# A graph network on one core: where the deferred rows of the second stage are kept, and the order in which its queues load and store at the start

## The chip, the core and the metric

The kernel runs on one of the eight cores of a Trainium2 chip. The metric is the device time of one execution in microseconds; a version is judged by the median of several executions. The core has five engines with an instruction queue each: TensorE (matmuls; PE in the profile), VectorE (DVE), ScalarE (ACT), GpSimd (POOL) and SyncE (SP), which here only issues transfers. SP, ACT and POOL can all issue transfers.

## What is computed

There are 10,000 nodes with 512 features and 160,000 edges, sorted by target, of four types. Two graph layers are computed, each with a normalised input and a residual:

```python
h = relu(layernorm(x))
# layer 0
msg = (einsum('nd,rdf->nrf', h, rel_W) + rel_b)[src, edge_type]
agg = segment_sum(msg, dst) / max(deg, 1)
x1  = layer_norm(h + h @ self_W + self_b + agg) * ln1_w + ln1_b
f   = gelu(x1 @ W1 + b1) @ W2 + b2
x   = x + layer_norm(x1 + f) * ln2_w + ln2_b
# layer 1: two SAGE layers on h = relu(layernorm(x))
h = relu(h @ W_self1 + mean_of_neighbours(h) @ W_neigh1 + b1)
h = relu(h @ W_self2 + mean_of_neighbours(h) @ W_neigh2 + b2)
x = x + h
```

W1 is 512 x 1024 and W2 is 1024 x 512. The call to `setup_inputs()` gives random features, edges and weights.

## The kernel before

Nodes are worked on in 79 blocks of 128 rows (`P`); the last block, 78, has 16 rows. There are four stages, each of them one loop over the blocks.

The **message stage** (lines 585 to 820) computes for each pair of blocks the four messages of every node and stores them in `hall_d`. It also computes the self term `h @ self_W + self_b` (with the identity added to the weights, so that it holds the residual too) and stores it in `xs_d`. For 24 blocks, 52 to 75, listed in `late`, the self term is not computed there: `residual` (line 698) stores the transposed block to `hT_d` instead (line 705), and the next stage makes up for it. Lists of edges are made beside this stage, on all engines, in pools of their own.

The **feed-forward stage** (from line 912, in `aligned`) is the middle one and the subject of this document. For each block it gathers rows of messages by indirect transfers from GpSimd (line 844, 256 KB each): up to 5 "others" tiles which TensorE adds up through 0/1 matrices (`hots`, `sums`, line 897), and 11 "mine" tiles, which VectorE adds one after the other (line 908). Blocks that begin a span of 4 or 16 blocks gather another tile, a tail; it is split into an upper and a lower half by VectorE and ScalarE (`halves_of`, lines 834 to 837). Every gathered tile comes from one ring of 28 tiles, `row_tile()`. A tile of the ring can be written again when its last use in program order is done.

After the sums of a block come its scale and residual (line 1181), its statistics, the first normalisation (lines 1081 to 1088), and the transposition for the feed-forward product (line 1016). The feed-forward products run one group of blocks behind: block 78 is a group, then groups of four. A group's 8 "up" slices (line 1028, then a Gelu on ScalarE into `hid`, line 1030) and its "down" products (line 1039) are put into `queue`, and one part of it is worked off in each round of the block loop, between the sums of two blocks. So the first two rounds have no feed-forward products to do.

The **deferred rows** are put into this gap. `fetch(n)` loads the next n blocks of `hT_d` (line 968), each into one tile of the ring. `residuals(n)` multiplies the oldest n of those loaded by `wself` (line 977, 4 matmuls of 512 columns each, which appear as 8 instructions in the trace), adds the bias on VectorE in place (line 979) and stores the row to `xs_d` (line 980). `LATE` says how many are fetched at each of its calls: the first two before the loop, the others in rounds 0 to 4. `ready` holds the ones that were fetched in the current round, which are left for the next one; `products` (line 1142) begins with two deferred rows, then does the part of the queue with the transposition in its middle, and ends with the rest of the rows.

The order of the work is the program's order on every engine: `aligned` runs under a manual schedule, each engine's queue is worked off in order, and waits are put in where tiles are written, read and used again. The transfers of SyncE are one such queue: a store that waits for its result holds back every load behind it. Before the loop, SyncE's order is: four deferred rows, the first two blocks of `xs_d`, the four stores of deferred rows, constants (`ln1w`, `lnb2`, `b2s` and two columns), four more deferred rows, `w1s`, `b1s`, `ln2w`. `w2s` is loaded in round 1.

Memory: the pools of a stage are laid out one after the other above the constants, on the place of the pools of the stage before: the ring `gat`, the weights `wp2`, the stage's tiles `gp` (with `hid`, 16 KB a partition, among them), and small ones, `sp`.

The **last two stages** (from line 1212) are the two SAGE layers, with the same gathers from `h1_d` and `h2_d`. The first of their gathers needs every row of `h1_d`, so it begins when the feed-forward stage has stored its last block.

Of the kernel before, what the change touches and what calls it, by code (L numbers as in the profile page):

```python
# [16 lines left out]
P = 128  # L17
# [4 lines left out]
def kernel(  # L22
# [789 lines left out]
    def aligned(ctxa):  # L812
# [98 lines left out]
        with ExitStack() as s:  # L911
            ring.append((s.enter_context(tc.tile_pool(name="gat", bufs=1)), RINGS[0]))
            wp = s.enter_context(tc.tile_pool(name="wp2", bufs=1))
            gp = s.enter_context(tc.tile_pool(name="gp", bufs=1))
            sp = s.enter_context(tc.tile_pool(name="sp", bufs=3))
            psT = s.enter_context(tc.tile_pool(name="psT2", bufs=1, space=PSUM))
            psC = s.enter_context(tc.tile_pool(name="psC", bufs=1, space=PSUM))
            psH = s.enter_context(tc.tile_pool(name="psH", bufs=2, space=PSUM))
# [36 lines left out]
                                  allow_slow_non_contiguous=True)  # L955
                return t

            LATE = (4, 4, 4, 3, 3, 3, 3)
            assert sum(LATE) == len(late)
            halves = [wself[:, :2], wself[:, 2:]]  # L960
            waiting, arrived = list(late), []

            def fetch(n):

                for b in waiting[:n]:
                    i = late.index(b)
                    t = row_tile()
                    nc.sync.dma_start(t, hT_d[i * P:(i + 1) * P, :])
                    arrived.append((b, t))
                del waiting[:n]  # L970

# [8 lines left out]
                    nc.sync.dma_start(xs_d[b * P:(b + 1) * P, :], t)  # L980
                del arrived[:n]

            fetch(LATE[0])
            for b in blocks[:2]:
                load(b)
            lanes = psC.tile([P, D], F32, name="lanes")[:, :P]
            nc.scalar.copy(lanes, lane)
            first_hot = hots(blocks[0], gp, lanes)
            residuals(LATE[0])
            ln1w = wide(wp, ln1_w, D, "ln1w")  # L990
            lnb2 = wide(wp, ln1_b, D, "lnb2")
            b2s = gp.tile([P, 2, D], F32, name="h1", bufs=2)[:, 0, :]
            nc.sync.dma_start(b2s, bass.AP(tensor=b2.tensor, offset=b2.offset,
                                           ap=[[0, P], [1, D]]))
            ln1wc, ln1bc = column(ln1_w, "ln1wc"), column(ln1_b, "ln1bc")
            fetch(LATE[1])
            nc.sync.dma_start(w1s, w1.rearrange("(k p) n -> p k n", p=P))
            nc.sync.dma_start(b1s, b1.rearrange("(f p) -> p f", p=P),
                              allow_slow_non_contiguous=True)
            ln2w = wide(wp, ln2_w, D, "ln2w")  # L1000
            taken = []

            class Group:
# [18 lines left out]
                def up(self, f):  # L1022
                    n = len(self.bs) * self.r
                    if self.hid is None:
                        self.hid = gp.tile([P, FC, 4 * P], F32, name="hid")
                    ph = psH.tile([P, 4 * P], F32, name="ph")
                    for k in range(KC):
                        nc.tensor.matmul(ph[:, :n], w1s[:, k, f * P:(f + 1) * P],  # L1028
                                         self.xT[:, k, :n], start=(k == 0), stop=(k == KC - 1))
                    nc.scalar.activation(self.hid[:, f, :n], ph[:, :n], AF.Gelu,  # L1030
                                         bias=b1s[:, f:f + 1], scale=1.0)
# [109 lines left out]
            def products(work, turned):  # L1141


                nonlocal fed
                got = []
                residuals(2)
                for i, call in enumerate(work):
                    if i == len(work) - 1:
                        yield
                    if i == len(work) // 2 and turned:  # L1150
                        turned()
                    got.append(call())
                if not work:
                    yield
                    if turned:
                        turned()
                residuals(len(arrived) - len(ready))
                fed = [g for g in got if g]
# [3 lines left out]
            for bs in plan:  # L1162
                for b in bs:
# [6 lines left out]
                        hot = hots(blocks[i + 1], gp, lanes)  # L1170
                    ready = []
                    if i + 2 < len(LATE):
                        fetch(LATE[i + 2])
                        ready = arrived[-LATE[i + 2]:]
                    if i == 1:
                        nc.sync.dma_start(w2s, w2.rearrange("(k p) n -> p k n", p=P))
                    got = second()
# [424 lines left out]
```

## Time and profile before

| | us |
|---|---|
| median of the runs | 7042.43 (7034.37, 7042.43, 7061.51) |
| the profiled execution | 6174.73 |
| its span, first to last instruction | 6172.9 |
| TensorE busy in it | 5643.4 |
| GpSimd busy (gathers) | 3722.7 |
| VectorE busy | 3671.8 |
| ScalarE busy | 1799.6 |
| last matmul of the message stage begins | 1206.43 |
| first gather of the feed-forward stage begins | 1206.87 |
| its last gather begins | 2853.8 |
| first gather of the next stage begins | 2949.35 |

The profiled execution is 868 us shorter than the median of the runs; nothing in the page says where the others spend that time. Durations below are those of the profiled execution.

The page gives for each engine the time it is busy, and for each group of instructions a mean duration and the idle time before it with the one who ended it. A matmul instruction that is busy may still be slow: the rate that the clock's throttle granted stands in a row of its own. Time of GpSimd is the time in which it makes the list for one gather; the data land later (3.8 us at the median). "Idle before" of an engine costs only where the engine, or one that waits for it, sets the end.

### The profile page before, as it was taken

The page shows a single profiled execution, that of the slowest core. Times are in us where ns is not written, and L with a number is a line of the kernel's source. Part 1 is how long each engine was busy: PE and PEld are TensorE (multiplying, and loading weights), DVE is VectorE, ACT ScalarE, POOL GpSimd, SP SyncE. Part 2 cuts the span into 40 slices and gives each one's busy share as a digit, 9 for nine tenths or more (in the row PEclk, how much of TensorE's full clock was granted, in tenths as well). Part 3 has the DMA queues.
Part 4 walks back from the last instruction along what each step waited for, and adds up shares of the span by engine and source line. Part 5 has one row for each costly group of instructions (what it writes and reads, how often), then busy time and mean ns, then how long its engine had stood idle before and what let it go on. Part 6 is the DMA issues. An engine that isn't in the chain of part 4 may idle for free.

```text
span 6172.9 us, 55148 instructions
## 1 busy us (share of the span) xinstructions
PE 5643.4 (91%) x15103; PEld 2563.5 (42%) x15103; DVE 3671.8 (59%) x7447; ACT 1799.6 (29%) x3594; POOL 3722.7 (60%) x3927
## 2 busy tenths in 40 slices
PE   9999999989999999999788888888878888888888
PEld 4555554444444444444333333333333333333333
DVE  8889999467877777775343434434334444444444
ACT  1026665013333333333222222222222222222222
POOL 0001110167777777773677777777767777777776
PEclk9999999999999999999999999999999999999999
DMA  4333344388888888885777777777778787888887
GB/s 161 116 124 128 122 145 150 139 282 253 263 259 262 262 253 258 253 260 164 232 235 238 234 238 234 237 237 235 238 235 251 246 251 247 250 251 246 251 246 218
DMA packets 503502, 1373.79 MB, mean 223 GB/s; under 512 B 82206, under 2 KB 82206, under 8 KB 503054
## 3 DMA queue, kind: packets, MB, share of 16 engines
q0 software_dynamic: 308768, 1008.91, 54.7%
q1 hardware_dynamic: 193886, 360.20, 16.0%
q8 instruction: 122, 2.00, 0.1%
q14 instruction: 198, 1.62, 0.1%
q10 hardware_dynamic: 528, 1.05, 0.0%
HBM read 1156.54 MB, written 213.30 MB: 222 GB/s over the span
## 4 chain that ended last, share of the span: by engine, by line
PE 40%; DMA 39%; DVE 8%; issue 6%; POOL 5%; ACT 1%; SPq 0%; POOLq 0%; DVEq 0%; ACTq 0%
DMA rows<-h_d,row 21%; PE pm L774 15%; DMA rows<-h_d,orow 13%; PE pa L897 6%; PE ph L1028 6%; POOL rows L844 5%; PE po L1039 5%; DMA rows<-hall_d,row 3%; DVE pa L908 3%; PE pm L678 2%; PE po L1273 1%; PE po L977 1%; PE pT L172 1%; DVE st L1066 1%; PE po L1244 1%
## 5 line engine op out<-in xcount | busy, mean ns | idle before, releaser
L908 DVE TENSOR_TENSOR pa<-pa,rows 128x512 f32<-128x512 f32 x2574 | 1798.8, 699 | 2042.1 <-PE pa L897 1236.7
L844 POOL DMA_INDIRECT rows<-h_d,row x1716 | 1622.2, 945 | 522.7 <-issue 283.6
L897 PE MATMUL pa<-rows,hot 128*128 128x512 f32 (+1 forms) x2358 | 1231.1, 637 | 348.0 <-DMA rows<-h_d,orow 314.2
L844 POOL DMA_INDIRECT rows<-hall_d,row x858 | 828.2, 965 | 269.8 <-issue 95.0
L844 POOL DMA_INDIRECT rows<-h_d,orow x786 | 743.0, 945 | 349.5 <-DMA h_d<-h 94.6
L897 PEld LDWEIGHTS pa<-rows,hot 128*128 128x128 f32 (+1 forms) x2358 | 403.3, 192 | 1114.6 <-DMA rows<-h_d,orow 838.7
L844 POOL DMA_INDIRECT rows<-hall_d,orow x393 | 372.6, 948 | 348.6 <-PE pm L678 203.4
L1273 PE MATMUL po<-wss,hTb 128*128 128x512 f32 (+1 forms) x1264 | 579.5, 602 | 0.0
L1039 PE MATMUL po<-w2s,hid 128*128 128x512 f32 (+1 forms) x1264 | 564.0, 600 | 15.4 <-DVE rest L1102 12.3
L1244 PE MATMUL po<-wns,mTb 128*128 128x512 f32 (+1 forms) x1264 | 572.2, 596 | 1.3 <-ACT mTb L173 1.3
L1028 PE MATMUL ph<-x1T,w1s 128*128 128x512 f32 (+2 forms) x1344 | 557.8, 568 | 2.6 <-ACT hid L1030 2.6
L173 ACT COPY mTb<-pT 128x512 f32<-128x512 f32 (+1 forms) x158 | 91.8, 581 | 1222.9 <-PE pT L172 1222.9
L1269 ACT ACTIVATE mb<-pa,rdeg 128x512 f32<-128x512 f32 (+1 forms) x158 | 108.5, 687 | 1140.7 <-DVE pa L908 1136.5
L879 PE MATMUL pa<-wss,ident 128*128 128x512 f32 x936 | 427.5, 593 | 0.0
L513 POOL DMA_INDIRECT win<-rec_d,at x79 | 81.4, 1030 | 528.5 <-PE pe L538 348.7
L1244 PEld LDWEIGHTS po<-wns,mTb 128*128 128x128 f32 (+1 forms) x1264 | 240.0, 190 | 307.3 <-issue 270.9
L1028 PEld LDWEIGHTS ph<-x1T,w1s 128*128 128x128 f32 x1344 | 249.0, 191 | 279.4 <-issue 273.2
L1039 PEld LDWEIGHTS po<-w2s,hid 128*128 128x128 f32 (+1 forms) x1264 | 237.2, 191 | 304.2 <-issue 281.3
L897 PE MATMUL pa<-tail,hot 128*128 128x512 f32 x624 | 308.0, 611 | 49.4 <-DMA tail<-h_d,srow 40.3
L866 ACT ACTIVATE hot<-lane,loc 128x128 f32<-128x128 f32 x1098 | 337.7, 391 | 0.0
L1273 PEld LDWEIGHTS po<-wss,hTb 128*128 128x128 f32 (+1 forms) x1264 | 233.7, 195 | 236.3 <-issue 235.5
L774 PE MATMUL pm<-wrel,hT 128*128 128x512 f32 x624 | 296.5, 598 | 0.0
(304 smaller groups left out, 6293.6 us busy)
## 6 DMA issues: line engine op xcount, KB each, us to landing
hall_d<-p SPq DMA_DIRECT2D x156, 256.0 KB, 2.5
hall_d<-u SPq DMA_DIRECT2D x156, 256.0 KB, 2.5
hb<-h_d SPq DMA_DIRECT2D x156, 256.0 KB, 4.2
rows<-h_d,row POOLq DMA_INDIRECT x1716, 3.8
xg<-in_x_dram SPq DMA_DIRECT2D x39, 512.0 KB, 3.6
xr_d<-xg SPq DMA_DIRECT2D x39, 512.0 KB, 2.8
xs<-xs_d SPq DMA_DIRECT2D x39, 512.0 KB, 8.5
h_d<-h SPq DMA_DIRECT2D x39, 512.0 KB, 4.4
```

What stands on the lines that cost most here:

```text
L678: nc.tensor.matmul(pm, a[:, k, :], w[:, k, :], start=(k == 0), stop=(k == KH - 1))
L774: nc.tensor.matmul(pm, a[:, k, :], w[:, k, :], start=(k == 0), stop=(k == KH - 1))
L844: nc.gpsimd.indirect_dma_start(out=t[:n], out_offset=None, in_=table, in_offset=bass.IndirectOffsetOnAxis(ap=idx, axis=0))
L866: nc.scalar.activation(hot[:, t, :], lane, AF.Abs, bias=loc[:, b, t:t + 1], scale=-1.0)
L879: nc.tensor.matmul(p, ident, w, start=True, stop=True)
L897: nc.tensor.matmul(pa[:r], h, v, start=(i == 0), stop=(i == len(work) - 1))
L908: nc.vector.tensor_tensor(pa[:r], pa[:r], t[:r], op=OP.add)
L1028: nc.tensor.matmul(ph[:, :n], w1s[:, k, f * P:(f + 1) * P], self.xT[:, k, :n], start=(k == 0), stop=(k == KC - 1))
L1039: nc.tensor.matmul(po[:r], self.hid[:, f, c * r:(c + 1) * r], w2s[:, f, :], start=(f == 0), stop=(f == FC - 1))
L1244: nc.tensor.matmul(po[:r], mT[:, k, :r], wns[:, k, :], start=False, stop=(k == KC - 1))
L1269: nc.scalar.activation(m[:r], pa[:r], AF.Copy, scale=rdeg[:r, b:b + 1])
L1273: nc.tensor.matmul(po[:r], hT[:, k, :r], wss[:, k, :], start=(k == 0), stop=False)
```

## The change

A pool `hp` is opened after `sp`, and `hid` moves there from `gp`. Its 8 slots of 512 columns (`FC` is 8) are at first used for eight deferred rows, which are fetched before the loop in one call by transfers issued from ScalarE's queue; the ring is used for the other sixteen, fetched on SyncE's queue as before. The first group's `hid` takes the place afterwards.

`LATE` becomes `(4, 0, 4, 4, 4, 3, 4, 1)`, and it now counts the rows that are *done* in each step: 4 before the loop, none in round 0, then 4, 4, 4, 3, 4 and 1 in rounds 1 to 6. Since the rows of the first three entries are all there before the loop, round 0 fetches nothing; rounds 1 to 5 fetch for the round behind them. `products` begins with two rows only where there are two that are not in `ready`.

Ahead of the loop, `residuals` of the first four rows moves from in front of the constants to behind `ln2w`, so that on SyncE's queue the constants and `w1s` come before the four stores; `ln1w` moves behind `b2s`. The second call of `fetch` is gone.

```diff
+            hp = s.enter_context(tc.tile_pool(name="hp", bufs=1))
...
-            LATE = (4, 4, 4, 3, 3, 3, 3)
-            assert sum(LATE) == len(late)
+            LATE = (4, 0, 4, 4, 4, 3, 4, 1)
+            EARLY = 8
+            assert sum(LATE) == len(late) and sum(LATE[:3]) == EARLY <= FC
...
-            def fetch(n):
+            def fetch(n, room=None):
-                for b in waiting[:n]:
+                for k, b in enumerate(waiting[:n]):
                     i = late.index(b)
-                    t = row_tile()
-                    nc.sync.dma_start(t, hT_d[i * P:(i + 1) * P, :])
+                    t = row_tile() if room is None else room[:, k, :]
+                    queue = nc.sync if room is None else nc.scalar
+                    queue.dma_start(t, hT_d[i * P:(i + 1) * P, :])
                     arrived.append((b, t))
                 del waiting[:n]
...
-            fetch(LATE[0])
+            fetch(EARLY, hp.tile([P, FC, D], F32, name="hid"))
             for b in blocks[:2]:
                 load(b)
             lanes = psC.tile([P, D], F32, name="lanes")[:, :P]
             nc.scalar.copy(lanes, lane)
             first_hot = hots(blocks[0], gp, lanes)
-            residuals(LATE[0])
-            ln1w = wide(wp, ln1_w, D, "ln1w")
             lnb2 = wide(wp, ln1_b, D, "lnb2")
             b2s = gp.tile([P, 2, D], F32, name="h1", bufs=2)[:, 0, :]
             nc.sync.dma_start(b2s, bass.AP(tensor=b2.tensor, offset=b2.offset,
                                            ap=[[0, P], [1, D]]))
+            ln1w = wide(wp, ln1_w, D, "ln1w")
             ln1wc, ln1bc = column(ln1_w, "ln1wc"), column(ln1_b, "ln1bc")
-            fetch(LATE[1])
             nc.sync.dma_start(w1s, w1.rearrange("(k p) n -> p k n", p=P))
             nc.sync.dma_start(b1s, b1.rearrange("(f p) -> p f", p=P),
                               allow_slow_non_contiguous=True)
             ln2w = wide(wp, ln2_w, D, "ln2w")
+            residuals(LATE[0])
...
-                        self.hid = gp.tile([P, FC, 4 * P], F32, name="hid")
+                        self.hid = hp.tile([P, FC, 4 * P], F32, name="hid")
...
-                residuals(2)
+                residuals(min(2, len(arrived) - len(ready)))
...
                     ready = []
                     if i + 2 < len(LATE):
-                        fetch(LATE[i + 2])
-                        ready = arrived[-LATE[i + 2]:]
+                        if i:
+                            fetch(LATE[i + 2])
+                        ready = arrived[len(arrived) - LATE[i + 2]:]
```

## The prediction, made before the changed kernel was run

> **What bounds the kernel now.** I read the page first (one core, clock 0.98, so nothing is disturbed), then the engines' timelines from the end of the message stage to the seventh round of the feed-forward stage, then a table of stretches, the waits and the instructions of the gather line. A round i is one pass of the block loop: round 0 is the block of 16 rows (78), round 1 is block 0. In each fence the columns are start, duration, engine, line, operation, tiles, count, and in brackets the idle time before and who ended it. TensorE:
>
> ```profile
> 1206.43 1.03 PE L678 MATMUL pm<-wself,s 128*128 128x256 f32 x4
> 1215.29 15.78 PE L977 MATMUL po<-wself,rows 128*128 128x512 f32 x32 [7.83 <-DMA rows<-hT_d]
> 1231.00 2.75 PE L897 MATMUL pa<-rows,hot 128*16 128x512 f32 x6
> 1246.16 15.70 PE L977 MATMUL po<-wself,rows 128*128 128x512 f32 x32 [12.42 <-DMA rows<-hT_d]
> ...
> 1277.54 8.52 PE L977 MATMUL po<-wself,rows 128*128 128x512 f32 x16 [3.24 <-DVE rows L979]
> ...
> 1342.40 8.43 PE L1039 MATMUL po<-w2s,hid 128*16 128x512 f32 x16 [3.15 <-DVE rows L979]
> ...
> 1370.13 6.57 PE L977 MATMUL po<-wself,rows 128*128 128x512 f32 x8 [3.15 <-DVE rows L979]
> ```
>
> The reader sees five holes, 29.8 us together, and nothing like them later. The matmuls after a hole are slow too: 32 take 15.78 us, while 16 take 6.87 in undisturbed rounds, so 32 should take 13.74. Summed over the six slow groups to round 6 (2.0, 2.0, 1.5, 1.8, 1.4, 3.0) this is 11.7 us. All that TensorE could win back here is 41.5 us. Next, why the second hole is there: SyncE's queue.
>
> ```profile
> 1207.95 0.37 SPq L725 DMA_DIRECT2D xs_d<-hg  x1
> 1209.08 1.93 SPq L968 DMA_DIRECT2D rows<-hT_d  x4
> 1211.46 1.05 SPq L937 DMA_DIRECT2D xs<-xs_d  x2
> 1221.52 10.62 SPq L980 DMA_DIRECT2D xs_d<-rows  x4
> 1232.19 0.42 SPq L145 DMA_DIRECT2D ln1w<-in_L_gnn_ln_w_dram  x1
> ```
>
> The four stores of deferred rows wait for their results until 1232.1, and behind them stand every constant, the next four rows (issued at 1235.94) and w1. GpSimd pays for it later:
>
> ```profile
> 1239.08 0.95 POOL L844 DMA_INDIRECT rows<-hall_d,row  x1 [0.30 <-issue]
> 1264.39 1.15 POOL L844 DMA_INDIRECT rows<-hall_d,orow  x1 [24.37 <-ACT upper L837]
> 1265.85 0.94 POOL L844 DMA_INDIRECT rows<-hall_d,orow  x1 [0.30 <-issue]
> ```
>
> Gathers normally follow each other every 1.25 us (0.95 and 0.30). The ring of 28 row tiles was empty of free ones until the split of block 0's tails (DVE, then the ACT copy, 1264.64) freed some, and that split stood in DVE's program order behind the four late residuals of round 0. After 1357 no wait of GpSimd in this stage is longer than about 0.3 us: 1276 gathers (858, 393 and 25) at 1.25 us are 1595 of the 1647 us from the first (1206.87) to the last (2853.8). So gathers pace this stage, with TensorE close behind (from 1385 to 2840 only 46 us of waits). What counts is therefore time lost by GpSimd in the ramp: beyond 0.30 each, 24.1 in the big wait, 4.8 in three waits on stores of deferred rows (2.43, 1.28, 1.96), 1.0 at 1333 and 2.7 at 1357, together 32.6 us.
>
> **What the skill says.** "Perfetto Trace Analysis", section "Optimizing DMA Performance", calls a kernel DMA-bound also when the issuing sequencer is solid with DMA work; GpSimd's 1.25 us rhythm is that. "TensorE: Matmul & The Clock Gate", section "Part 1: The HAM clock gate", says idle windows of about 3.4 us halve the matmul clock; the trace shows 0.66 granted in 1210 to 1220 and 0.52 in 1240 to 1250. "DMA: Bandwidth & Descriptors", section "Issuing engines are not separate DMA queues", says that transfers from SP, ACT and POOL share 16 engines and that another issuer saves only sequencer time. The trace agrees: in 1210 to 1220 the share is 1.01 at 342 GB/s. So ScalarE's queue is worth what it lets go earlier, not bandwidth.
>
> **Part 1, eight rows from ScalarE's queue into hid.** In the trace ScalarE ends the message stage at 1174.58 and runs the new stage's copy of lanes directly:
>
> ```profile
> 1173.99 0.59 ACT L173 COPY hT<-pT 128x512 f32<-128x512 f32 x1 [11.83 <-PE pT L172]
> 1174.62 0.27 ACT L987 COPY lanes<-lane 128x128 f32<-128x128 f32 x1
> ```
>
> The source rows were last written at 1150.41. Whether hid's memory is free I work out from tile sizes: weights, x tiles and work tiles of the message stage fill about 118 KB above the constants; the ring, weights and the other stage tiles come to about 172 KB; hid is the 16 KB above that, where only the edge lists' pools reached, whose DVE work ends at 1042.9. So eight issues of 0.48 us (1.93/4) start near 1174.6; behind them ScalarE has only the copy of lanes, wanted at 1208.7. Four rows took 6.08 us to land on busier engines; eight are there well before 1207 (DMA share 0.17 in 1180 to 1200). The first hole (7.83) goes, and so does its slow clock (2.0): four residuals run 1208.0 to 1221.8. If hid's memory is not free, both stay: cost 0 to 9.8; I take 0.
>
> **Part 2, constants and w1 ahead of the stores.** SP passes fetches and stores: from about 1210, xs 1.05, lnb2, b2, ln1w (0.43 each), two columns 2.2, w1 0.66, b1 0.93, ln2w 7.65, free by about 1225; the four stores follow, nobody waiting. DVE's add of lnb (L1139) has its data when DVE comes to it at 1222.5. What is late instead: w1's 2 MB now lands amid the first gathers (from 1215). At 350 GB/s (10 us stretches reach 342 to 389) some 9.9 MB of gathers, constants and stores take 28 us from 1208, so landings lag by 0 to 6 us near 1225; I take 1 to 2 at the point where it is felt.
>
> **Part 3, no residuals in round 0.** DVE goes on at 1222.5: add 0.7, masks 1.1, then block 78's chain (0.74, 0.69, 0.17, ScalarE's 0.29 and 0.77, 0.31, 1.5) to about 1230, and the tails' split to 1232. TensorE does block 78's sums 1221.8 to 1224.6 and block 0's by 1235, where before it ended at 1267. The second hole shrinks to some 5 us of waiting for gathers. GpSimd: 3 tiles for block 78 and 20 for block 0 fit into 28 without a wait, so the waits on stores and the 24.37 go; block 1's slots come free at 1232 to 1236, before GpSimd asks for them at 1235 to 1254.
>
> **Part 4, rounds 1 to 6 carry 4, 4, 4, 3, 4, 1 rows instead of 4, 3, 3, 3, 3, 0.** A row is 8 matmuls, 3.44 us. A round costs sums 5.2 and rows 13.7; rounds 2 and 3 have 4.1 more, round 4 has 6.9 of down products. The third row of a round still waits for DVE's 11 additions in rounds 1, 4 and 5: 3.2 and 1.5 of slow clock each, as before. So sums start at 1254 (round 2), 1277, 1300, 1327.5, 1351.6 (round 6, before 1376.1): 24.5 ahead with one row (3.4) still to do, 21 net. GpSimd in rounds 3 to 6 meets slots held by the fourth row's store (landing 3.9): waits of 1.5, 1.4, 2.6, about 6 us. Its gain is 32.6 - 6 = 26.6. The chain runs through both; I take 23.
>
> **Part 5, edits at nothing.** hid in its own pool: the first Gelu into it needs the eight stores landed. The last leaves at 1253 and lands by 1257; the Gelu comes at 1265, with ScalarE's later copies queued behind it: cover 8 us, beyond that one for one. The last rows' loads and later stages are unchanged: TensorE's drain after the last gather and the wait of the next stage for the last h1 store only move.
>
> **Sum.** 6174.7 - 23 = 6152 for the profiled execution. The timed median, 7042.4, is 868 us above it and no view shows why; matmuls slower by a fifth would give holes of 28 before and 7 after (21), slower gathers about the same stall, so I subtract the same 23: 7019.
>
> **Rivals.** A, as worked out: 10 to 35 us gained, 7007 to 7032. B, only the first hole goes, because four rows a round make TensorE the pace of the ramp (23.1 us a round against 20 of gathers): 9.8 gained, 7033. For: the share of TensorE; against: it is ahead by 31 us in round 2. C, gathers never wait and TensorE's holes close fully: about 38, 7004. Against: the additions of DVE still end before the third row. D, slower: in rounds 2 to 6 up to eight tiles of the ring hold deferred rows, so only 20 are left for 16 gathers a round; if every round then runs at 23.1 instead of 20 (five times 3.1, 15 us) and every store adds its wait (2.6 a row for rounds 2 to 5, 15 rows, 39), the 54 exceed the 32.6 plus the clock (11.7) saved by about 9: 7051. It decides from 44 us of such waits on. For: three such waits are in the trace now; against: they are 4.8 us.
>
> **Chances.** A 0.70, B 0.12, C 0.10, D 0.08. The range takes A's, most of B and C, and the spread of the shown runs (7034 to 7062): 6999 to 7040. A difference under 0.5%, 35 us, is about what a measurement cannot tell from none: faster 0.23 (C, and A's upper end with the scatter), same 0.71, slower 0.06.
>
> **What would show it.** ScalarE's eight issues near 1175; TensorE's residuals at 1208 with no hole; GpSimd without the 24.37 us wait; block 0's sums ending near 1235; round 6 near 1352; the next stage's first gather near 2926 (2949.35 now). Wrong if the issues come after 1207, if GpSimd waits over 15 us in rounds 2 to 6, or if later rounds give the lead back.

## The result, and the profile after

The changed kernel took 7049.1 us (median of 14 runs), the kernel before 7049.0 (14 runs): a ratio of 0.9997, 95% interval 0.9987 to 1.0008. A second comparison in a later batch gave 0.9983 (0.9970 to 0.9997). The forecast was 7019, 23 us less than before, with a range of 6999 to 7040.

The study's runs fell on chips of two kinds, on which the same program differs by some 870 us: the kernel before took 7055.5, 7057.8 and 7041.6 us in three of its comparisons (two chips) and 6176.5 and 6179.2 in two (two other chips). The mean clock granted to TensorE was 0.90 on the slower ones and 0.98 on the faster. The profile from which the prediction was read (6174.7) belongs to the faster kind, the runs printed beside it (7042) and both comparisons above to the slower. On the faster kind the changed kernel was run later, as the experiment e12_after: 6164.3 against 6179.2, a ratio of 0.9974 (0.9963 to 0.9985), so 15.0 us gained. Two of the fourteen executions of the last experiment, e18, were disturbed (7219 and 8135 us) and are left out of its ratio. The lines of e12_after can be laid beside those of the prediction. TensorE's timeline comes first (start, duration, line, operation, and in brackets the idle time before it and who ended it):

```profile
1206.28 1.03 PE L678 MATMUL pm<-wself,s 128*128 128x256 f32 x4
1208.02 13.97 PE L980 MATMUL po<-wself,hid 128*128 128x512 f32 x32 [0.71 <-DVE hg L680]
1221.92 7.45 PE L897 MATMUL pa<-rows,hot 128*16 128x512 f32 x16
...
1244.26 8.83 PE L980 MATMUL po<-wself,hid 128*128 128x512 f32 x16 [2.77 <-DVE hid L982]
...
1266.71 0.63 PE L1018 MATMUL pT<-ident,xs 128*128 128x128 f32 x4
1273.16 3.59 PE L1030 MATMUL ph<-x1T,w1s 128*128 128x16 f32 x16 [5.82 <-ACT hid L1032]
1276.60 10.01 PE L980 MATMUL po<-wself,rows 128*128 128x512 f32 x16
```

The two holes of 7.83 and 12.42 us are gone: the first four rows run from 1208.02 to 1221.99, and block 0's sums end by 1234. A new hole stands at 1273, of a kind that the kernel before did not have: TensorE's "up" products wait for ScalarE's write to `hid`. GpSimd's timeline:

```profile
1236.08 0.94 POOL L844 DMA_INDIRECT rows<-hall_d,orow  x1 [0.30 <-issue]
...
1279.20 0.94 POOL L844 DMA_INDIRECT rows<-hall_d,orow  x1 [2.17 <-DVE pa L1088]
...
1286.72 0.94 POOL L844 DMA_INDIRECT rows<-hall_d,orow  x1 [5.32 <-DMA xs_d<-rows]
...
1309.39 0.94 POOL L844 DMA_INDIRECT rows<-hall_d,orow  x1 [4.04 <-DMA xs_d<-rows]
...
1341.26 0.94 POOL L844 DMA_INDIRECT rows<-hall_d,orow  x1 [5.16 <-DVE lower L836]
```

The wait of 24.37 us is gone, and GpSimd gathers without a pause for 70 us; then it begins to wait, because the rounds whose tiles it needs have become late. The whole story is in one table: the time at which VectorE scales the sums of a round's block (line 1181 before, 1184 after), on the faster kind of chip, from one trace of each version. Row 78 is the block loop's last round.

| round | before | changed (e12_after) | lead | rows 4 to 14 not in `hid` (e13_hid_free) | rows per round as before (e11_parts12) |
|---|---|---|---|---|---|
| 0 | 1242.8 | 1224.7 | 18.1 | 1225.8 | 1223.8 |
| 1 | 1275.2 | 1241.9 | 33.3 | 1243.1 | 1251.0 |
| 2 | 1299.4 | 1266.4 | 33.0 | 1267.6 | 1275.5 |
| 3 | 1318.9 | 1299.9 | 18.9 | 1292.2 | 1298.4 |
| 4 | 1340.0 | 1324.5 | 15.5 | 1318.5 | 1319.6 |
| 6 | 1390.0 | 1378.3 | 11.7 | 1371.0 | 1369.9 |
| 8 | 1428.8 | 1420.5 | 8.3 | 1413.2 | 1408.7 |
| 78 | 2858.3 | 2847.7 | 10.6 | 2841.4 | 2837.3 |

From round 8 on the lead of no column over the kernel before changes by more than 3 us. So what the stage wins is decided in its first eight rounds: 33 us are won by round 1, and 25 of them given back by round 8, 14 of these in round 3 alone. (The leads are between single executions. The profiled ones of before and e12_after differ by 11.9 us in the whole, near the 10.6 of the last row; their medians by 15.0.)

ScalarE's timeline shows what held round 3; SyncE's comes after it (for SyncE and for ScalarE's "ACTq" lines, durations are the time over which the issues were spread):

```profile
1189.51 19.17 ACTq L971 DMA_DIRECT2D hid<-hT_d  x8
1208.72 0.27 ACT L990 COPY lanes<-lane 128x128 f32<-128x128 f32 x1 [34.31 <-DMA hid<-hT_d]
...
1245.78 1.12 ACT L1020 ACTIVATE x1T<-pT,ln1bc,ln1wc 128x16 f32<-128x16 f32 x4
1271.54 1.28 ACT L1032 ACT_TABLE_LOAD   x1 [24.64 <-DMA xs_d<-hid]
```

```profile
1222.69 8.27 SPq L145 DMA_DIRECT2D ln2w<-in_L_gnn_ln_w_dram  x1
1231.08 3.96 SPq L983 DMA_DIRECT2D xs_d<-hid  x4
1235.09 0.45 SPq L938 DMA_DIRECT2D xs<-xs_d  x1
1235.59 6.00 SPq L971 DMA_DIRECT2D rows<-hT_d  x4
1243.26 0.38 SPq L1179 DMA_DIRECT2D w2s<-in_L_gnn_W_dram  x1
1244.37 10.73 SPq L983 DMA_DIRECT2D xs_d<-hid  x4
```

ScalarE stands still for 24.64 us before the table load of its first Gelu, because that Gelu writes `hid`, where the rows 4 to 7 had lain, and their stores had not landed. They were issued by 1255.1 (1244.37 + 10.73), behind w2's 2 MB, and the wait ends at 1271.5, some 16 us later. Transfers are listed next (issues, size, median us from issue to landing), those of 1225 to 1290 first, then those issued from 1243 to 1254:

```profile
rows<-hT_d SPq DMA_DIRECT2D x11, 256.0 KB, 12.4
xs_d<-hid SPq DMA_DIRECT2D x8, 256.0 KB, 14.5
w2s<-in_L_gnn_W_dram SPq DMA_DIRECT2D x1, 2048.0 KB, 22.8
...
rows<-hall_d,row POOLq DMA_INDIRECT x32, 6.1
```

```profile
xs_d<-hid SPq DMA_DIRECT2D x4, 256.0 KB, 19.6
rows<-hall_d,row POOLq DMA_INDIRECT x10, 6.1
```

The four stores of rows 4 to 7 took 17.4 to 22.8 us. GpSimd's gathers are of the same size and landed in 6.1 us in the same stretch (6.0 in the kernel before), so it is not that every transfer was slow. In this trace SyncE's transfers land in the order in which they were issued: w2 at 1266.0 (1243.26 + 22.8), then the four stores from 1267.2 to 1271.3. They waited for what stood ahead of them in their own queue.

The windows by stage (us, then busy us and instructions of TensorE, its weight loads, VectorE, ScalarE and GpSimd, then granted clock, DMA share and GB/s) show how full the engines were, and a second price:

```profile
1230.00:1250.00 20.00, 15.51 (x34) 7.39 (x35) 15.33 (x25) 3.31 (x8) 15.12 (x17) 0.83 1.05 387
1250.00:1270.00 20.00, 17.34 (x58) 9.04 (x56) 12.59 (x19) 0.00 (x0) 15.13 (x17) 0.97 1.04 394
1270.00:1290.00 20.00, 16.84 (x43) 9.59 (x44) 4.22 (x7) 7.30 (x13) 9.36 (x11) 0.69 0.69 241
```

The DMA engines are full from 1230 to 1270; ScalarE does nothing from 1250 to 1270; and in the 20 us after that TensorE, back from its hole, is granted 0.69 of its clock: two rows take 10.01 us instead of 7.03 (0.70).

### The profile page after: what moved, and what is told of

Read it like the earlier page. It is cut to its first block, busy times and chain, and to the rows that moved or that the text cites. A ratio compares the mean times of both kernels' runs of the same rounds, so it can differ in the third digit from the quotient of the medians.

```text
span 7030.1 us, 55146 instructions
## 1 busy us (share of the span) xinstructions
PE 5756.5 (82%) x15103; PEld 2675.2 (38%) x15103; DVE 3683.9 (52%) x7447; ACT 1805.0 (26%) x3594; POOL 3716.9 (53%) x3927
## 4 chain that ended last, share of the span: by engine, by line
PE 61%; issue 19%; another core or an unknown queue 9%; DVE 5%; ACT 3%; DMA 2%; POOL 2%; SPq 0%; POOLq 0%; DVEq 0%; ACTq 0%
PE pa L897 14%; PE pm L774 13%; PE ph L1030 7%; PE po L1247 7%; PE po L1041 6%; PE po L1276 4%; PE pa L879 4%; DVE pa L908 3%; PE pm L678 2%; POOL rows L844 2%; PE pT L172 2%; PE po L980 1%; DMA rows<-h_d,row 1%; PE pT L1018 0%
## 5 line engine op out<-in xcount | busy, mean ns | idle before, releaser
L1247 PE MATMUL po<-wns,mTb 128*128 128x512 f32 (+1 forms) x1264 | 737.9, 738 | 836.5 <-issue 653.0
L897 PE MATMUL pa<-rows,hot 128*128 128x512 f32 (+1 forms) x2358 | 1116.1, 613 | 101.1 <-issue 91.1
L1247 PEld LDWEIGHTS po<-wns,mTb 128*128 128x128 f32 (+1 forms) x1264 | 290.2, 238 | 1270.5 <-issue 1043.6
L897 PEld LDWEIGHTS pa<-rows,hot 128*128 128x128 f32 (+1 forms) x2358 | 456.1, 194 | 706.6 <-issue 680.9
L1030 PE MATMUL ph<-x1T,w1s 128*128 128x512 f32 (+2 forms) x1344 | 582.5, 585 | 74.1 <-ACT hid L1032 37.1
L1276 PE MATMUL po<-wss,hTb 128*128 128x512 f32 (+1 forms) x1264 | 596.3, 616 | 39.6 <-issue 24.5
L1041 PE MATMUL po<-w2s,hid 128*128 128x512 f32 (+1 forms) x1264 | 581.3, 609 | 47.2 <-issue 45.1
L774 PE MATMUL pm<-wrel,s 128*128 128x512 f32 x624 | 293.3, 592 | 0.0
L897 PE MATMUL pa<-tail,hot 128*128 128x512 f32 x624 | 293.2, 592 | 0.0
```

Source lines behind the costliest of these rows:

```text
L774: nc.tensor.matmul(pm, a[:, k, :], w[:, k, :], start=(k == 0), stop=(k == KH - 1))
L897: nc.tensor.matmul(pa[:r], h, v, start=(i == 0), stop=(i == len(work) - 1))
L1030: nc.tensor.matmul(ph[:, :n], w1s[:, k, f * P:(f + 1) * P], self.xT[:, k, :n], start=(k == 0), stop=(k == KC - 1))
L1041: nc.tensor.matmul(po[:r], self.hid[:, f, c * r:(c + 1) * r], w2s[:, f, :], start=(f == 0), stop=(f == FC - 1))
L1247: nc.tensor.matmul(po[:r], mT[:, k, :r], wns[:, k, :], start=False, stop=(k == KC - 1))
L1276: nc.tensor.matmul(po[:r], hT[:, k, :r], wss[:, k, :], start=(k == 0), stop=False)
```

## The experiments

All are compared with the kernel before, in runs of the same batch. The first four tell whether the ramp of the stage sets the end at all, and what each part does alone (slower kind of chip; before 7055.5).

**e0_before**, the kernel before, unchanged.

> The kernel before, unchanged, for a trace of an execution of the usual length (about 7045 us instead of 6175). Theory R (the gain is made and given back inside the ramp): TensorE's two holes of 7.8 and 12.4 us are there as in the trace that was read, block 0's sums end near 1267 us against 1232.8 in the changed kernel, but the sums of round 6 begin within 5 us of the changed kernel's 1390. Theory P (the ramp is not on the path): round 6 begins 15 us or more later than in the changed kernel, and the two meet later, so that the first gather of the next stage begins within 10 us of the changed kernel's. Theory U (the trace that was read was unusual): the holes of the ramp are not there.

It took 7065.7 us, with a span of 7064.0. Its ramp has the holes that the prediction read (7.65 and 11.32 us in TensorE, 23.89 in GpSimd), so these do not belong to the faster chip alone, and theory U falls. Round 6 is scaled at 1417.0, 9.7 us after that of the changed kernel's first profile (1407.4), between the 5 us of theory R and the 15 of theory P. What differs from the faster chip begins at round 2. Of the groups of instructions in the window 2000 to 2800 (count, busy us and mean ns, idle before and who ended it), the first fence is from the profile of the prediction, the second from e0_before:

```profile
L908 DVE TENSOR_TENSOR pa<-pa,rows 128x512 f32<-128x512 f32 x429 | 299.4, 698 | 95.5 <-DMA rows<-hall_d,row 79.1 <-PE pa L897 4.8
...
L1028 PE MATMUL ph<-x1T,w1s 128*128 128x512 f32 x640 | 281.2, 592 | 0.0
```

```profile
L908 DVE TENSOR_TENSOR pa<-pa,rows 128x512 f32<-128x512 f32 x356 | 248.8, 699 | 121.8 <-PE po L1039 55.5 <-remote 35.4 <-PE pa L897 9.7
...
L1028 PE MATMUL ph<-x1T,w1s 128*128 128x512 f32 x527 | 241.7, 610 | 24.9 <-ACT hid L1030 19.4 <-issue 5.4
```

The operations last as long (592 and 610 ns, 698 and 699), fewer are done in the same 800 us, and what VectorE waits for has changed from gathers to TensorE's results. From round 8 to the last a round takes 24.3 us instead of 20.4.

**e1_plus32**: 32 more matmuls (27.5 us) ahead of the first deferred rows.

```
             first_hot = hots(blocks[0], gp, lanes)
+            keep_busy(psO.tile([P, D], F32, name="po"), wself[:, 0, :], 32)
             residuals(LATE[0])
```

> The kernel before with 32 matmuls of 512 columns more on TensorE, ahead of the first deferred rows (their result is not used; 64 instructions of 0.43 us, 27.5 us of TensorE in the ramp). Theory P: the ramp is not on the path, the time rises by less than 8 us. Theory R and theory U: TensorE's order in the ramp sets the end, and the time rises by 12 to 28 us (7.8 us of it fill the first hole).

1.0031 (1.0013 to 1.0050), some 22 us slower, 9 to 35 by the interval (the medians differ by 10). Work put ahead of the first rows arrives at the end, if not whole: the ramp is on the path, and theory P falls.

**e2_early8**: part 1 alone, eight rows from ScalarE's queue into `hid`, four of them done before the loop and four in round 0.

```
-            fetch(LATE[0])
+            fetch(LATE[0] + LATE[1], hp.tile([P, FC, D], F32, name="hid"))
...
-            fetch(LATE[1])
```

> Part 1 of the change alone: eight deferred rows from ScalarE's queue into hid's place; constants, stores and the rows of each round (4 before the loop, then 4, 4, 3, 3, 3, 3) as before. Theory R: it has the first hole's gain (about 10 us) and most of the second hole's (the rows are there in round 0), and with 4 and 3 rows a round as before it does not give it back: 10 to 25 us faster. Theory P: within 6 us of before.

0.9986 (0.9974 to 0.9998), some 10 us gained, the lower end of what theory R said.

**e3_stores_last**: part 2 alone, `residuals(LATE[0])` and `ln1w` moved behind the other constants as in the change.

```
-            residuals(LATE[0])
-            ln1w = wide(wp, ln1_w, D, "ln1w")
...
             ln2w = wide(wp, ln2_w, D, "ln2w")
+            residuals(LATE[0])
```

> Part 2 alone: the four stores of deferred rows go behind the constants, w1 and ln2w on SyncE's queue; rows fetched by SyncE as before. Theory R: the second hole shrinks (four rows are fetched some 15 us earlier), 5 to 12 us faster. Theory P: within 6 us of before.

0.9987 (0.9971 to 1.0003), some 9 us gained, though the interval touches 1. Two parts with about 10 us each, and a whole with 0: that put the new schedule of rows under suspicion. The next four ask about it (slower kind; before 7057.8).

**e4_parts12**: the changed kernel with the rows per round of before.

```
-            LATE = (4, 0, 4, 4, 4, 3, 4, 1)
+            LATE = (4, 4, 4, 3, 3, 3, 3)
...
-                        if i:
-                            fetch(LATE[i + 2])
+                        fetch(LATE[i + 2])
```

> The whole change without its new row schedule: eight rows by ScalarE's queue into hid, constants, w1 and ln2w ahead of the stores, and rows done 4, 4, 4, 3, 3, 3, 3 as before (so round 0 keeps its four). Theory G (the new schedule of rows gives the early gain back, because rounds 1 to 4 carry four rows each, whose ring tiles and stores hold GpSimd): the two gains of about 10 us seen alone (7045.0 and 7044.3 against 7055.5) add up, 15 to 20 us below the kernel before, and below the changed kernel. Theory H (the two parts win the same microseconds, and whatever the order, rounds 1 to 4 are held by the same thing, the 16 DMA engines that gathers, rows, w1 and w2 share): about 10 us below before, no better than the parts alone. In both, the sums of round 0 end later than in the changed kernel; under G round 8 leads the kernel before by 20 us or more, under H by about 14 to 27, as the parts alone do.

0.9970 (0.9956 to 0.9983): 20 us gained. The two parts add up, and the version is ahead of the change.

**e5_schedule**: the kernel before with `LATE = (4, 0, 4, 4, 4, 3, 4, 1)` alone.

> The kernel before with the new row schedule alone (4 rows ahead of the rounds, none in round 0, then 4, 4, 4, 3, 4, 1), rows still fetched by SyncE into ring tiles, constants still behind the stores. Theory G: 5 to 20 us slower than before, with waits of GpSimd on stores of rows or on the sums of over 40 us in rounds 1 to 6. Theory H: within 5 us of before. The prediction's own reckoning (part 3 alone: the 24 us wait goes, some waits on stores come): 5 to 20 us faster.

0.9993 (0.9978 to 1.0009). Theory H's number; not the 5 to 20 us of loss of theory G, nor the gain that part 3 of the prediction gives by itself.

**e6_light**: the changed kernel with `LATE = (4, 0, 4, 3, 3, 3, 3, 3, 1)`.

> The changed kernel with a flatter tail: 4, 0, 4, 3, 3, 3, 3, 3, 1 rows (eight rounds after the first instead of six). Theory G: GpSimd's waits on stores of rows in rounds 2 to 4 (11.75 and 9.27 in the changed kernel) shrink, and it comes out 5 to 15 us below the changed kernel. Theory H: the same as the changed kernel within 5 us, since round 1 still has four rows beside w1 and w2.

0.9985 (0.9970 to 0.9999), 2 us below the changed kernel beside it. No wait of GpSimd of over 2 us on a store of rows is left in its ramp, yet nothing is won: waits of 8.49, 9.20 and 7.42 us on TensorE's sums stand in their place. Theory H's number again.

**e7_after**: the changed kernel.

> The changed kernel itself, so that the three above can be read against it on the same chip. Both theories: level with the kernel before within 10 us (7049.1 against 7049.0 so far). If it is 10 us or more below, the level result so far is a matter of the chip, and nothing was given back.

0.9983 (0.9970 to 0.9997), 10 us below before, 9 above e4_parts12. Together with the first comparison (0) the change is worth some 0 to 10 us on this kind of chip.

The next four went to a chip of the faster kind (before 6176.5), where runs of one kernel lie closer together.

**e8_rest**: deferred rows out of the ring.

```
-                    t = row_tile() if room is None else room[:, k, :]
+                    if room is not None:
+                        t = room[:, k, :]
+                    elif i < EARLY + 11:
+                        t = gp.tile([P, D], F32, name="rest", bufs=11)
+                    else:
+                        t = row_tile()
```

> The changed kernel with deferred rows 8 to 18 fetched into the eleven 'rest' tiles, which nobody uses before the first down products, in place of ring tiles; rows 19 to 23 stay in the ring. Theory G1 (the new schedule gives the gain back because deferred rows hold ring tiles until their stores have landed): GpSimd's waits on stores of rows in rounds 2 and 3 (11.75 and 9.27 us; 13.09 and 10.90 in the second profile) go, the ramp is 10 to 20 us shorter, and the time falls to 15 to 25 us below the kernel before, level with the version of parts 1 and 2. Theory G2 (TensorE is what the later rows press: the tiles only wait because the products come late): the waits on stores turn into waits on TensorE, and the time stays within 5 us of the changed kernel (about 10 below before).

0.9978 (0.9969 to 0.9987), 12 us gained, no more than the changed kernel on this kind (15): theory G2's number. The waits on stores are gone from GpSimd's timeline, and these stand there:

```profile
1313.52 0.95 POOL L844 DMA_INDIRECT rows<-hall_d,row  x1 [10.38 <-PE pa L897]
1342.06 0.94 POOL L844 DMA_INDIRECT rows<-hall_d,row  x1 [10.12 <-ACT upper L837]
```

GpSimd is ahead by a ring of tiles, so it feels a late round only when the ring is used up, and its wait is then put down to whoever frees the next tile. Taking that releaser away changed the name, not the time: theory G1, and with it the mechanism of rival D, is not what held the ramp on this kind of chip.

**e9_parts12_rest**: the same in the version of parts 1 and 2.

> The version of parts 1 and 2 (rows 4, 4, 4, 3, 3, 3, 3) with rows 8 to 18 in the 'rest' tiles as well. Theory G1: its one wait on a store of rows (8.17 us) goes, and it is 5 to 10 us better than without, 25 to 30 below before. Theory G2: the same as without it, about 20 below before.

0.9972 (0.9962 to 0.9983), 18 us gained, against 23 without it. G1 misses here too.

**e10_half**: half of the products of the later rows left out (its result is not that of the kernel).

```
+                    ks = KC if late.index(b) < 4 else KC // 2
-                    for k in range(KC):
+                    for k in range(ks):
...
-                                         start=(k == 0), stop=(k == KC - 1))
+                                         start=(k == 0), stop=(k == ks - 1))
```

> The changed kernel with half of the products left out (two of four 128-row slices) in the 20 deferred rows after the first four, so that TensorE has 80 matmuls, some 34 us, less to do in rounds 1 to 6; tiles, stores and DMAs as they were. Theory G1: GpSimd's waits on stores of rows stay at least half as long, the time is at most 10 us below the changed kernel. Theory G2: 20 to 34 us below the changed kernel (30 to 45 below before), the waits gone.

0.9964 (0.9951 to 0.9978), 22 us gained, so only some 7 better than the change for 34 us of matmuls less. Both theories missed. The timeline of TensorE shows what ate the rest: a hole of 13.25 us before the "up" products at 1272.85, "<-ACT hid". TensorE came there earlier, and the Gelu did not (its table load began at 1271.22, against 1271.54 in the changed kernel). That is the wait on `hid` again.

**e11_parts12**: e4_parts12 again.

> The version of parts 1 and 2 once more, beside the three above. If its lead is real, 12 to 28 us below the kernel before as in the first look (0.9970, 0.9956 to 0.9983); if it was scatter, within 10 us.

0.9964 (0.9950 to 0.9977), 23 us gained; all five runs lie between 6153.0 and 6154.6. Here the rows 4 to 7 are done in round 0. Their stores are issued by 1243.5 instead of 1255.1, and ahead of w2 (1246.91). They land in 6.7 us at the median, and the first Gelu's table load (1256.0) has no wait.

The next four (faster kind; before 6179.2) test theory G3.

**e12_after**: the changed kernel; its profile is the one shown above.

> The changed kernel itself, for the three beside it. Both theories: 5 to 15 us below the kernel before, behind the version of parts 1 and 2 (20 and 23 below). Its lead over the kernel before is largest in round 1 (33 us) and under 20 us from round 4 on.

0.9974 (0.9963 to 0.9985), 15 us gained, 8 less than parts 1 and 2; the leads are in the table.

**e13_hid_free**: rows 0 to 3 in `hid`, 4 to 14 in the "rest" tiles.

```
-                    t = row_tile() if room is None else room[:, k, :]
+                    if i < 4:
+                        t = room[:, k, :]
+                    elif i < 15:
+                        t = gp.tile([P, D], F32, name="rest", bufs=11)
+                    else:
+                        t = row_tile()
```

> The changed kernel with only rows 0 to 3 in hid, rows 4 to 14 in the 'rest' tiles (4 to 7 still from ScalarE's queue ahead of everything) and rows 15 to 23 in the ring. Theory G3 (the first Gelu into hid waits for the stores of rows 4 to 7, which lay in hid, are now done in round 1 and land late; ScalarE and then TensorE stand still meanwhile): that wait goes, since rows 0 to 3 are stored by about 1245, round 3 comes 8 us or more earlier than in the changed kernel and in the version with rows 8 to 18 in 'rest', and the time is 18 to 30 us below before. Theory G2 (four rows a round are more than TensorE and VectorE can carry beside the sums): within 5 us of the changed kernel.

0.9956 (0.9942 to 0.9969): 24.6 us gained, 9.7 more than the change. Its five runs (6148.4 to 6157.6) lie below all seven of e12_after (6160.5 to 6167.7). ScalarE and TensorE at the place in question:

```profile
1248.12 1.28 ACT L1037 ACT_TABLE_LOAD   x1
1267.21 0.27 ACT L1037 ACTIVATE hid<-ph,b1s 128x16 f32<-128x16 f32 x1 [17.81 <-PE ph L1035]
```

```profile
1267.92 0.63 PE L1023 MATMUL pT<-ident,xs 128*128 128x128 f32 x4
1268.39 1.86 PE L1035 MATMUL ph<-x1T,w1s 128*128 128x16 f32 x16
1270.09 8.81 PE L985 MATMUL po<-wself,rest 128*128 128x512 f32 x16
```

The table load comes 23 us earlier, ScalarE now waits for TensorE and not the other way round, and the hole of 5.82 us is gone. Round 3 is at 1292.2 instead of 1299.9 (expected: 8 us earlier or more). The stores of rows 4 to 7 land as late as before (18.4 us at the median), but no longer out of `hid`. That rows 8 to 14 left the ring as well is not what paid: e8_rest took rows 8 to 18 out of it and gained no more than the change.

**e16_w2_late**: the changed kernel with w2's load in round 2 (`if i == 2`).

> The changed kernel with the 2 MB load of w2 issued in round 2 in place of round 1. Theory G3: the stores of rows 4 to 7 then share the DMA engines with less and land some 8 us sooner; the first Gelu into hid starts sooner by as much, and the time is 4 to 10 us below the changed kernel. Theory G2: the same as the changed kernel within 3 us.

0.9954 (0.9940 to 0.9968). Four of five runs are between 6150.3 and 6153.1, 12 us below the changed kernel (expected: 4 to 10); the profiled one is the fifth, 6168.8, and even it shows the effect in its ramp (round 3 at 1293.5, though its stage began 2 us later). Stores out of `hid` landed in 10.2 us at the median instead of 14.5, those of rows 4 to 7 in 9.3 instead of 19.6, and:

```profile
1261.26 1.28 ACT L1032 ACT_TABLE_LOAD   x1 [11.91 <-DMA xs_d<-hid]
1268.44 0.27 ACT L1032 ACTIVATE hid<-ph,b1s 128x16 f32<-128x16 f32 x1 [5.90 <-PE ph L1030]
```

The wait is still there, but it ends before anyone needs the Gelu. So either edit takes away the wait and is worth about the same, 24.6 and 26 us: one price, on `hid` and on the load ahead of its stores. That the load costs nothing by itself is not shown: both edits together were not run on this kind of chip.

**e14_schedule**: e5_schedule on this kind of chip.

> The new row schedule alone once more (no row in hid, constants behind the stores as before), beside the changed kernel. Theory G3: no wait on hid exists here, so the schedule is worth what part 3 gives, 5 to 15 us below before. Theory G2: within 5 us of before, as in the first look (0.9993).

0.9991 (0.9983 to 1.0000), 4 us. Nearer to theory G2's number than to G3's. In the traces its round 1 leads that of before by 12.3 us and its round 8 trails by 5.1: four rows taken out of round 0 (4 times 3.44 us, 13.8) come back as work in later rounds.

The last two (slower kind again; before 7041.6) ask whether these are one price or two, and for the best version.

**e17_parts12_w2_late**: e4_parts12 with w2's load in round 2.

> The version of parts 1 and 2 (rows 4, 4, 4, 3, 3, 3, 3), where the rows in hid are stored by about 1250 and the first Gelu does not wait, with w2 loaded in round 2. Theory G3 (the load matters only because it delays the stores that hold hid): as without it, 18 to 28 us below before. If the load costs by itself (gathers or rows arriving late), 3 to 8 us better than that.

0.9950 (0.9938 to 0.9963), 37 us gained, the best of all. That is more than expected under either reading, and it was run on the slower kind alone; why the later load is worth so much there I did not find out.

**e18_hid_free_w2_late**: e13_hid_free with w2's load in round 2.

> The changed kernel with rows 4 to 14 in the 'rest' tiles and w2 loaded in round 2. Theory G3: one price, taken away once: 22 to 30 us below before, within 4 us of either edit alone. If they are two prices: 30 to 36 below.

0.9995 (0.9986 to 1.0004), 3 us: a clear miss. On this kind of chip something else takes the gain, and freeing `hid` with w2 late doesn't bring it back. VectorE's timeline:

```profile
1250.48 0.69 DVE L987 TENSOR_TENSOR rest<-po,bself 128x512 f32<-128x512 f32 x1 [6.89 <-remote]
1272.17 0.69 DVE L987 TENSOR_TENSOR rest<-po,bself 128x512 f32<-128x512 f32 x1 [21.00 <-remote]
```

These are the additions to the first and second deferred rows of round 1; the records of their matmuls end at 1237.8 and 1241.2. TensorE's third and fourth rows need the two `po` buffers that they free, and wait 9.65 and 15.67 us. The changed kernel's first profile has the same on TensorE and VectorE:

```profile
1254.69 6.48 PE L980 MATMUL po<-wself,hid 128*128 128x512 f32 x8 [12.96 <-issue]
1265.96 5.97 PE L980 MATMUL po<-wself,hid 128*128 128x512 f32 x8 [4.79 <-DVE hid L982]
```

```profile
1242.49 0.18 DVE L1069 BATCH_NORM_AGGREGATE mv<-st 128x2 f32<-128x6 f32 x1
1253.95 0.69 DVE L982 TENSOR_TENSOR hid<-po,bself 128x512 f32<-128x512 f32 x1 [11.28 <-issue]
1265.21 0.69 DVE L982 TENSOR_TENSOR hid<-po,bself 128x512 f32<-128x512 f32 x1 [10.57 <-remote]
```

e7_after (4.61 and 6.70 us of TensorE) and e6_light (4.58 and 12.99) show the same two holes; e4_parts12 has one of 2.22 us before the third row of that round, e17_parts12_w2_late one of 1.29. On the faster kind the changed kernel has 2.77 us there. These holes are in every trace of the changed loads with the new schedule on this kind of chip, but how much of the time they make up is not shown. The changed kernel's two traces scale round 8 at 1457.6 and 1447.4, and that of e4_parts12, whose runs were 9 us shorter, at 1448.2; e5_schedule, the new schedule with the old loads, has only 3.16 us of hole there and gains no more. That VectorE starts late because TensorE's results reach it late is the reading that fits, but no run settles why that happens on this kind of chip, nor why the order with four rows in round 0 is spared.

## Why the prediction was right and wrong

**Part 1** was right in its effect and wrong in its time. TensorE's rows start at 1208.02 with no hole, as said. But ScalarE's first issue comes at 1189.5, not near 1174.6, and the last at 1208.4, later than the 1207 that the prediction had named as a sign of being wrong. The semaphore events of the trace tell what the first four waited for: issues at 1189.51, 1193.42, 1201.54 and 1205.78 follow, by 0.02 us each, the landing of a message store (`hall_d`) that counts its completion on the same semaphore. The next three, whose semaphores were free, come 0.48 us apart (1206.15 to 1207.12), as the prediction took for all. It cost nothing only because the first four were enough for the start. Alone the part gained 10 us, the number of its working (7.8, and 2.0 of slow clock); but in that trace the second hole shrinks too (4.77 instead of 11.32) and waits of 4.03 and 9.40 us come in round 2, so the number doesn't prove the working.

**Part 2** was right in direction: SyncE is free at 1231 (said: 1225), and alone it gained about 9 us. Its side effect was mis-sized: "landings lag" was taken at 1 to 2 us, from bytes over bandwidth, as if every transfer shared alike. From 1225 to 1290 SyncE's rows and stores took 12 to 15 us, and in e14_schedule, without the early weights, 5.3 to 5.4; the gathers took 6.1 and 6.0. The place in the Trainium skill that the prediction names, "DMA: Bandwidth & Descriptors", section "Issuing engines are not separate DMA queues", says that transfers of all issuers interleave on the same engines; the share of 1.05 at 387 GB/s agrees, but it doesn't tell how long one transfer waits. In this trace that depended on what stood ahead of it in its queue.

**Part 3** was right nearly to the microsecond: block 0's sums end near 1234 (said: 1235), the 24.37 us go. But parts 1 and 2 do most of that without it: in e11_parts12 the longest wait of GpSimd is 8.05 us, and it gains 23 us with the old rows per round. So part 3, with the rounds that pay for it, added 2 us at most (24.6 in e13_hid_free), which the scatter doesn't tell from none.

**Part 4** was right for the faster kind: the rounds of e13_hid_free, where part 5's wait is absent, follow its reckoning to within 6 us. Adding the 14 us that lie between the start of sums and the scale in the profile of before (1376.1 to 1390.0, round 6), it says 1268, 1291, 1314 and 1366 for rounds 2, 3, 4 and 6; measured 1267.6, 1292.2, 1318.5 and 1371.0. GpSimd's waits on stores of rows, put at 6 us, were about 9 in the two longest (5.32 and 4.04).

**Part 5** is the step that failed for the faster kind: "The last leaves at 1253 and lands by 1257; the Gelu comes at 1265 ...: cover 8 us." The last store was issued at 1253.9, as said, and landed at 1271.3: 17.4 us where 4 had been taken from the profile of before. There the stores of round 0 were issued before w2's load. The new schedule, part 3 itself, moves rows 4 to 7 into round 1 and so puts their stores behind w2's 2 MB in SyncE's queue; the prediction counted w1's bytes but nothing for w2. In e11_parts12, with the same constants and w1 but the old schedule, the same four stores go ahead of w2 and land in 6.7 us at the median. TensorE stood still for 5.82 us, and slower matmuls after the hole (3.59 for 1.86 and 10.01 for 8.81) made it 8.9 us from round 2 to round 3, against e13_hid_free; the medians of the two differ by 9.7, their profiled executions by 5.3. The prediction had named the price beyond the cover ("one for one"). With this wait the sum is 23 less some 10, so 13; measured 15. Without it, 24.6 were measured where 23 had been said. That this comes so near is in part luck: e11_parts12 reaches 23 without parts 3 and 4, and the next stage's first gather in the trace of e13_hid_free is at 2932.5 (said: 2926), 16.9 us earlier than before.

**The sum** is the step that failed in the runs that were forecast, those of the slower kind: "I subtract the same 23" from a median 868 us above the profile. That was a wager on an unexplained difference. There the change is worth 0 to 10 us. Part 5's wait is not what took the rest: ScalarE does wait for `hid` in both traces of the changed kernel (6.94 and 6.77 us), but until 1274.94 and 1271.64, before TensorE's "up" products begin (1283.85 and 1274.15). What those traces show in its place are the holes of 11.3 and 17.8 us before the third and fourth row of round 1 (25.3 in e18_hid_free_w2_late), which the profile of the faster kind had given no reason to expect. Their cause, and how much of the loss is theirs, stay open.

Of the rivals, D had the right sign of doubt (deferred rows that hold tiles others need, and stores that land late), in the wrong place: it laid the price on the ring, where e8_rest shows that it isn't; on the faster kind it lay on `hid`. The sign that the prediction gave, "GpSimd waits over 15 us in rounds 2 to 6", did come on the slower kind (11.75 and 9.27 us on stores of rows, with 14.57 on sums), but as the mark of a late round: with a flatter schedule (e6_light) those waits go and nothing is won.

## What to carry to other kernels

A tile borrowed ahead of its owner is given back when the last store out of it has landed, not when it was issued; take that landing time from what the change puts ahead of the store in its own queue (here 2 MB, 17 to 23 us instead of 4), not from the old profile. Work moved out of the first round is a loan: it makes the first round look 33 us better, and has to be carried by rounds that may have less room. And where the profile and the timed runs disagree by 14%, find out which of the two the change will be timed on before moving a number from one to the other.

The version that beats both kernels is the change without its new schedule (e4_parts12 and e11_parts12): 0.9970 (0.9956 to 0.9983) on the slower kind of chip and 0.9964 (0.9950 to 0.9977) on the faster; with w2 loaded a round later 0.9950 (0.9938 to 0.9963) on the slower, and not run on the faster.

## What the runs showed of the hardware

- Two kinds of chip, 870 us apart with one program, with operations of nearly the same duration; the mean clock granted to TensorE is 0.90 and 0.98. On the slower kind VectorE's additions to the first two rows of round 1 start 12.7 to 31.0 us after the recorded end of their matmuls (the changed kernel's first profile and e18_hid_free_w2_late); to the rows ahead of the loop they start 0.04 us after it. Whether TensorE or the records are late stays open.
- A transfer issued from ScalarE waited for the landing of an earlier one, issued from SyncE, that counts on the same semaphore: four issues came 0.02 us after such landings, 3.9 to 8.1 us apart; with free semaphores three came 0.48 us apart.
- Stores of 256 KB behind a 2 MB load in SyncE's queue took 17.4 to 22.8 us to land, while gathers of 256 KB issued from GpSimd took 6.1 us in the same stretch, at 387 to 394 GB/s in all. With the load issued after them the stores of the same rows took 6.7 (e11_parts12) and 9.3 (e16_w2_late) at the median. The load itself took 20 to 23 us from issue to landing in the versions of the change, 16.7 in the kernel before.
